# Column sums of image 0's group 0: Pool additions instead of accumulating transfers, and one lane-us more ahead of the sums of image 3's first normalization

## The chip, the cores and the metric

The kernel runs on one core of one Trainium2 chip. The metric is the device time of one execution in microseconds; lower is better. All numbers are for fp32 data.

## The reference

The input x holds four images of 64 x 64 positions with 64 channels. Four layers follow one another:

```python
# layer 0: self-attention over the 4096 positions of an image
q, k, v = x @ Wq + bq, x @ Wk + bk, x @ Wv + bv
x = gamma * einsum('bmn,bmc->bnc', softmax(q @ k.T), v) + x
# layer 1: a gated convolution block
y = dw3x3(ln(x) @ pw1 + b); y = y1 * y2; y = y * (mean(y) @ sca + b)
x = x + (y @ pw2 + b) * beta
z = ln(x) @ pw3 + b; x = x + ((z1 * z2) @ pw4 + b) * gamma
# layer 2: attention of the image with itself, no weights
x = softmax(xf.T @ xf) applied to xf, + x
# layer 3: attention with 32 inner channels, then a normalization over the batch
f = softmax(theta(x) @ phi(x).T); w_y = (f @ g(x)) @ W + b
x = x + gamma * (w_y - mean) / sqrt(var + eps) + beta
```

Layer 1 thus has two normalizations over channels for every image (`ln`). In layer 2 the score matrix is symmetric, so that a tile of exponentials computed once can be used a second time, transposed.

## The kernel before, in words

**Order of the work.** Everything runs on one core. The order on TensorE, ScalarE, VectorE and Pool is the order in which the program issues it (a manual schedule). `items` is a list of steps: layer 0 of images 0 to 3 (32 items each), then layer 2 of image 0, then layer 2 and layer 3 of the images in turn. Two *lanes* run beside the items, `conv` (layer 1 of an image) and `misc` (projections, features). A lane is a list of generators. A generator issues some instructions and yields a number of lane-us; the lane issues its next step when its clock, which the items advance by `tick`, has come that far. So a larger yield puts all later steps of a lane later among the items:

```python
def step(self):
    try:
        self.next = max(self.next, self.now - 8.0) + next(self.gens[0])
```

Layer 1 of image 3 begins 34 items after the start of its layer 0, that is in the first items of layer 2 of image 0. There an item advances `conv` by 3.3 lane-us, and by 1.5 in seven items marked `slow`.

**Layer 2 of image 0.** The positions fall into eight groups h of 512. For image 0 the list `PART` gives the tiles of each group; group 0 comes first. Each item n computes one tile of 128 x 1024: four score matmuls (L1391) into a PSUM slot, two exponentials on ScalarE (L1396) into half of a buffer `e` (pool `ep`, six buffers of 2048 columns), and some items later four product matmuls (L1452). Tiles listed in a pair are used twice. For these,

- `turned` transposes the tile on VectorE (L1409) into `turned`;
- `column_sums` adds the tiles of the group: two sums in the halves of a buffer `esum`, by transfers from Pool's queue that accumulate (L1425), one more transfer that adds the halves (L1429), and an addition of 512 columns on Pool (L1433);
- three items after the last tile of a pair `turned_products` issues 64 matmuls (L1478), written to two PSUM slots, and VectorE copies or adds them to `A` (L1493 where `A` is new, else L1491), which frees the slots;
- nine items after the group's last tile `spread_sums` reads `esum` on VectorE (L1441, L1442).

Group 0 has eight such tiles, items 4 to 7 and 10 to 13; group 1 has four, groups 6 and 5 have eight each. In the other images `column_sums` adds on Pool (L1431), and only there.

Three PSUM slots of 1024 columns are in turn for everything here: L1391, L1478 (two at once), and layer 1's matmuls (L1206).

**Layer 1 of image 3, first part.** `norm` squares x on ScalarE (L1165), sums over channels on TensorE (L1171), computes the inverse deviation (L1176, L1177, L1179, L1180), spreads it over the channels by eight transfers on SP's queue (L1184) into `xn`, and multiplies it by x in two halves on VectorE (L1192). Then come four pointwise matmul groups (L1206), each evacuated by ScalarE into `pad` (L1223), and the 3 x 3 taps: the first of nine on ScalarE (L1237), the rest on VectorE (L1241, L1244), for the second half of the channels. A second pass over the same `pad` does the first half (L1206, L1223, L1237, L1241, L1252), and L1258, L1261, L1263, L1265 and L1270 close the block. The second normalization and the second pointwise pair (L1206, L1289, L1291, L1295, L1298) follow.

The yield between the second square and the sums is `first - 2.5` lane-us.

Of the kernel before, what the change touches and what calls it, by code (L numbers as in the profile page):

```python
# [691 lines left out]
def fast_path(ctx: ExitStack, tc: tile.TileContext, a: dict, out: bass.AP, bad):  # L692
    nc = tc.nc
    B, H, W, C = a["x"].shape
# [31 lines left out]
    def new_ps():  # L726
        if turn_of["banks"]:
            if turn_of["bank"] % turn_of["banks"] == turn_of["banks"] - 1:
                turn_of["bank"] += 1
            k = new_bank(), new_bank()  # L730
            return PS[:, 512 * k[0] : 512 * k[0] + 1024]
        s = turn_of["slots"][turn_of["ps"] % len(turn_of["slots"])]
        turn_of["ps"] += 1
        return PS[:, bass.ts(s, 1024)]
# [13 lines left out]
    def new_e(name="e"):  # L748
        return ep.tile([128, 2048], F32, tag="e", name=name)

    def new_t(name="t"):
        return tp.tile([128, 1024], F32, tag="t", name=name)

    def new_big(name):
        return big.tile([128, 4096], F32, tag="big", name=name)
# [404 lines left out]
    def norm(x, y, first, more):  # L1160


        sq = [new_t("sq"), new_t("sq")]
        for i in range(2):
            act(sq[i], x[:, bass.ts(i, 1024)], AF.Square)  # L1165
            yield first - 2.5 if i else 2.5
        ps = new_ps()
        for i, src in enumerate(((x, x), (sq[0], sq[1]))):
            for j in range(4):
                c = 512 * j if i == 0 else 512 * (j % 2)  # L1170
                mm(  # L1171
                    ps[32 * j : 32 * j + 32, bass.ts(i, 512)], jsel, src[j // 2][:, c : c + 512],
                    start=True, stop=True,
                )
        t = new_t()
        act(t[:, 0:512], ps[:, 0:512], AF.Square)  # L1176
        stt(t[:, 0:512], t[:, 0:512], -1.0, ps[:, 512:1024], ALU.mult, ALU.add)  # L1177
        yield 4.0
        act(t[:, 0:512], t[:, 0:512], AF.Ln, bias=eps1)  # L1179
        act(t[:, 512:1024], t[:, 0:512], AF.Exp, scale=-0.5)  # L1180
        yield 3.0
        for j in range(4):
            for h in range(2):
                nc.sync.dma_start(  # L1184
                    out=y[64 * h : 64 * h + 64, bass.ts(j, 512)],
                    in_=t[32 * j + 16 * h : 32 * j + 16 * h + 16, 512:1024]
                    .unsqueeze(1).to_broadcast([16, 4, 512]),
                )
        yield 11.0 + more
        for jp in range(2):  # L1190
            cols = bass.ts(jp, 1024)
            nc.vector.tensor_mul(y[:, cols], y[:, cols], x[:, cols])  # L1192
            yield 1.8
# [6 lines left out]
    def layer1(b):  # L1200
        x = X[:, b]
# [8 lines left out]
                    )  # L1210

        y = xn.tile([128, 2048], F32, tag="xn", name="xn")
        yield from norm(x, y, 4.5, 3.0 if b == B - 1 else 0.0)
        yg = new_big("yg")
        yw = yg.rearrange("c (s q p h) -> c p q s h", s=2, p=2, h=H)
        ysum = sm.tile([128, 8], F32, tag="ysum", name="ysum")
# [108 lines left out]
    def layer2(b, when_free=None):  # L1325


        x, m, first = X[:, b], im[b], len(items)
# [84 lines left out]
        def column_sums(n):  # L1413
            h, _, _, run, _ = steps[n]
            if run is None:
                return
            k, e = mine_t[h].index(n), st["e"][n]
            if k == (0 if b == 0 else 1):
                st["esum"][h] = new_e("esum")
            if h not in st["esum"]:  # L1420
                return
            esum = st["esum"][h][:, 0:1024]
            if b == 0:
                both = st["esum"][h]
                nc.gpsimd.dma_start(  # L1425
                    out=both[:, bass.ts(k % 2, 1024)], in_=e, **({} if k < 2 else {"accum_op": ALU.add})
                )
                if n == mine_t[h][-1]:
                    nc.gpsimd.dma_start(out=esum, in_=both[:, 1024:2048], accum_op=ALU.add)  # L1429
            else:  # L1430
                nc.gpsimd.tensor_add(esum, st["e"][mine_t[h][0]] if k == 1 else esum, e)  # L1431
            if n == mine_t[h][-1]:
                nc.gpsimd.tensor_add(esum[:, 0:512], esum[:, 0:512], esum[:, 512:1024])  # L1433
# [62 lines left out]
        def item(n):  # L1496
            if n in weights_at:
                weights(weights_at[n])
            score(n)
            turned(n)  # L1500
            column_sums(n)
            todo.append(n)
            if n == 2:
# [309 lines left out]
    for b in range(B):  # L1813
        if b:
            misc_to[len(items)] = True
        layer0(b)
        if b + 1 < B:
            gens = [load_x(i) for i in range(1, B)] if b == 0 else []
            misc_from[32 * b + 16] = gens + [project0(b + 1)]
        conv_from[32 * b + 34] = layer1(b)  # L1820
# [241 lines left out]
```

## Time and profile before

| | us |
|---|---|
| median of 3 runs | 2462.84 (2461.17 to 2462.88) |
| profiled execution, whole | 2460.35 |
| its span | 2458.5 |
| TensorE busy (share of the span) | 2419.4 (98%) |
| ScalarE busy | 1642.8 (67%) |
| VectorE busy | 1475.9 (60%) |
| Pool busy | 533.0 (22%) |
| granted TensorE clock, mean | 0.997 |
| L1425, 28 issues on Pool | 22.0 |
| L1431, 126 additions on Pool that read `esum` and `e` | 299.5 (2.377 each) |

The page gives times of one profiled execution. The span runs from its first to its last instruction; the whole execution is 1.85 us longer, and the median of the runs is 2.5 us above that. A line such as L1096 is a line of the kernel before. "Busy" of TensorE counts matmuls at whatever clock was granted, so a slow stretch looks busy. Layer 2 of image 0 lies between about 1025 and 1260 us of the span.

### The profile page before, as it was taken

How to read it: one execution, taken by the hardware profiler on the slowest of the kernel's cores; microseconds unless marked ns; L12 is line 12 of the kernel's file. 1: busy time of each engine (PE TensorE's matmuls, PEld its weight loads, DVE VectorE, ACT ScalarE, POOL GpSimd, SP SyncE). 2: the span in 40 equal slices, each digit the busy share in tenths (PEclk: the TensorE clock that was granted, in tenths of full speed). 3: DMA queues.
4: the chain of work that ended last, by engine and by line, in shares of the span. 5: the costliest groups of instructions: out<-in, count | busy, mean ns of one | idle time of the engine just before them, and what ended most of it. 6: DMA issues, size and time to landing. Idle time of an engine off the chain costs nothing.

```text
span 2458.5 us, 63660 instructions
## 1 busy us (share of the span) xinstructions
PE 2419.4 (98%) x27509; PEld 930.3 (38%) x27509; DVE 1475.9 (60%) x1794; ACT 1642.8 (67%) x3140; POOL 533.0 (22%) x383
## 2 busy tenths in 40 slices
PE   9999999999999999999999999999999999999998
PEld 3343453336333633335434442144431344421113
DVE  2010378227822773268656668876668866678886
ACT  4656766676666666668654459954479744579996
POOL 2000000000000000020136551255631365622110
PEclk9999999999999999999999999999999999999999
DMA  3000000000000000250540027610075400286554
GB/s 79 1 18 1 19 1 18 18 19 1 18 18 19 1 19 18 61 113 2 126 83 19 19 64 136 138 28 22 17 149 118 80 20 20 70 169 141 120 117 118
DMA packets 67669, 136.40 MB, mean 55 GB/s; under 512 B 13004, under 2 KB 34229, under 8 KB 67381
## 3 DMA queue, kind: packets, MB, share of 16 engines
q0 software_dynamic: 24320, 86.55, 17.4%
q1 hardware_dynamic: 42309, 43.85, 7.9%
q8 instruction: 218, 3.57, 0.6%
q10 hardware_dynamic: 752, 1.85, 0.2%
q14 instruction: 70, 0.57, 0.1%
HBM read 4.80 MB, written 4.19 MB: 4 GB/s over the span
## 4 chain that ended last, share of the span: by engine, by line
PE 87%; DVE 6%; ACT 4%; issue 1%; SPq 1%; DMA 1%; ACTq 0%; DVEq 0%
PE PS L1096 18%; PE PS L1122 18%; PE PS L1391 9%; PE PS L1452 9%; PE PS L1645 9%; PE PS L1706 8%; PE PS L1478 7%; PE PS L1206 2%; DVE tg L1697 2%; ACT e L1656 2%; ACT e L1396 1%; DVE X L1567 1%; PE PS L1560 1%; PE PS L1171 1%; PE PS L1295 1%
## 5 line engine op out<-in xcount | busy, mean ns | idle before, releaser
L1101 ACT ACTIVATE e<-PS 128x1024 f32<-128x1024 f32 x512 | 523.7, 1023 | 338.7 <-PE PS L1096 305.6
L1396 ACT ACTIVATE e<-PS 128x512 f32<-128x512 f32 x632 | 370.8, 595 | 342.4 <-PE PS L1391 321.5
L1096 PE MATMUL PS<-X,q 64*64 64x512 f32 x4096 | 573.6, 590 | 2.3 <-DVE X L979 1.7
L1122 PE MATMUL PS<-e,vq 64*64 64x512 f32 x4096 | 575.6, 592 | 0.0
L1656 ACT ACTIVATE e<-PS 128x512 f32<-128x512 f32 (+2 forms) x588 | 500.1, 921 | 59.4 <-PE PS L1645 37.9
L1697 DVE TENSOR_TENSOR tg<-tg,e 128x2048 f32<-128x2048 f32 x172 | 393.8, 2290 | 43.1 <-ACT e L1656 31.3
L1391 PE MATMUL PS<-ko 64*64 64x512 f32 x2528 | 340.5, 598 | 1.5 <-ACT ko L1313 0.8
L1452 PE MATMUL PS<-e,X 64*64 64x512 f32 x2528 | 334.8, 592 | 0.5 <-ACT own L1464 0.3
L1241 DVE SCALAR_TENSOR_TENSOR y<-pad,vec,y 128x1024 f32<-128x1024 f32 x240 | 309.8, 1291 | 18.7 <-ACT y L1237 11.3
L1431 POOL TENSOR_TENSOR esum<-esum,e 128x1024 f32<-128x1024 f32 x126 | 299.5, 2377 | 54.3 <-ACT e L1396 47.3
L1409 DVE STREAM_TRANSPOSE turned<-e 128x1024 f32<-128x1024 f32 x196 | 240.5, 1238 | 111.3 <-ACT e L1396 111.1
L1645 PE MATMUL PS<-tg,ph 32*64 32x512 f32 x4096 | 295.7, 613 | 1.7 <-ACT e L1656 0.8
L1096 PEld LDWEIGHTS PS<-X,q 64*64 64x64 f32 x4096 | 183.2, 133 | 261.5 <-issue 181.5
L1122 PEld LDWEIGHTS PS<-e,vq 64*64 64x64 f32 x4096 | 183.1, 133 | 253.7 <-issue 158.1
L1425 POOL DMA_DIRECT2D esum<-e x28 | 22.0, 785 | 1170.7 <-ACT e L1396 1066.7
L1706 PE MATMUL PS<-e,tg 128*32 128x512 f32 x2048 | 272.6, 604 | 0.0
L1109 DVE TENSOR_REDUCE sums<-zs 128x1 f32<-128x4 f32 x128 | 19.6, 153 | 276.2 <-ACT e L1101 276.0
L1452 PEld LDWEIGHTS PS<-e,X 64*64 64x64 f32 x2528 | 104.3, 133 | 168.4 <-issue 145.6
L1678 POOL DMA_DIRECT2D xn<-e x116 | 101.1, 904 | 292.4 <-ACT e L1656 204.6
L1391 PEld LDWEIGHTS PS<-ko 64*64 64x64 f32 x2528 | 97.2, 133 | 162.9 <-issue 138.0
L1645 PEld LDWEIGHTS PS<-tg,ph 32*64 32x64 f32 x4096 | 63.5, 130 | 223.3 <-ACT e L1656 190.9
L1396 ACT ACTIVATION_READ_ACCUMULATOR e<-PS 128x1 f32 x632 | 127.4, 202 | 0.0
(219 smaller groups left out, 1727.5 us busy)
## 6 DMA issues: line engine op xcount, KB each, us to landing
xn<-e POOLq DMA_DIRECT2D x132, 512.0 KB, 5.3
esum<-e POOLq DMA_DIRECT2D x28, 512.0 KB, 5.8
xn<-t SPq DMA_DIRECT2D x64, 128.0 KB
ph<-tg SPq DMA_DIRECT2D x64, 128.0 KB
xn<-X SPq DMA_DIRECT2D x224, 32.0 KB
xr<-X SPq DMA_DIRECT2D x176, 32.0 KB
ko<-ko SPq DMA_DIRECT2D x32, 128.0 KB
xr<-in_x_dram SPq DMA_DIRECT2D x13, 256.0 KB
```

The source lines that it names most:

```text
L1096: mm(ps[64 * c : 64 * c + 64, bass.ts(r, 512)], m.q[rows_, 128 * t + 64 * c : 128 * t + 64 * c + 64], x[rows_, bass.ts(g, 512)], start=Tru ...
L1101: act(es[g // 2][:, bass.ts(g % 2, 1024)], ps, AF.Exp, bias=SHIFT0, accum_out=zs[:, g : g + 1],)
L1122: ins = mm(PS[64 * s : 64 * s + 64, 2048 + 512 * j : 2560 + 512 * j], vq[rows_, :], es[j // 2][rows_, k : k + 512], start=t == 0 and i < 2 ...
L1241: stt(y1, win, wt, y1, ALU.mult, ALU.add)
L1391: mm(ps[64 * c : 64 * c + 64, bass.ts(r, 512)], m.ko[rows_, k : k + 64], m.ko[rows_, bass.ts(h, 512)], start=True, stop=True,)
L1396: act(e[:, bass.ts(r, 512)], ps[:, bass.ts(r, 512)], AF.Exp, bias=SHIFT2, accum_out=slot(g, 2 * u + r),)
L1431: nc.gpsimd.tensor_add(esum, st["e"][mine_t[h][0]] if k == 1 else esum, e)
L1452: mm(st["acc"][r][64 * c : 64 * c + 64, :], xw[rows_, 4 * g + 2 * u + c, :], st["e"][n][rows_, bass.ts(c, 512)], start=n == mine[h][0], st ...
L1645: mm(PS[64 * c : 64 * c + 64, bass.ts(banks[k], 512)], m.ph[32 * k : 32 * k + 32, 128 * mc + 64 * c : 128 * mc + 64 * c + 64], m.th[32 * k ...
L1656: act(e[:, 512 * lo : 512 * k], PS[:, 512 * banks[lo] : 512 * banks[lo] + 512 * (k - lo)], AF.Exp,)
L1697: nc.vector.tensor_add(esum, esum, e)
L1706: mm(st["y"][32 * k : 32 * k + 32, :], m.gx[:, i % 32, :], es[i][:, bass.ts(k, 512)], start=mc == 0, stop=i % 32 == 31,)
```

## The change

Group 0 of image 0 takes the path of the other images: its first tile issues nothing, its second allocates `esum` and adds the first two tiles on Pool, and the others are added one by one. Groups 1, 6 and 5 keep their transfers. In `norm` of image 3's first normalization, the yield ahead of the sums is 3.0 instead of 2.0 lane-us. Below L1417 every line of the changed kernel has a number one higher.

```diff
         y = xn.tile([128, 2048], F32, tag="xn", name="xn")
-        yield from norm(x, y, 4.5, 3.0 if b == B - 1 else 0.0)
+        yield from norm(x, y, 5.5 if b == B - 1 else 4.5, 3.0 if b == B - 1 else 0.0)
...
             k, e = mine_t[h].index(n), st["e"][n]
-            if k == (0 if b == 0 else 1):
+            moved = b == 0 and h > 0
+            if k == (0 if moved else 1):
                 st["esum"][h] = new_e("esum")
             if h not in st["esum"]:
                 return
             esum = st["esum"][h][:, 0:1024]
-            if b == 0:
+            if moved:
                 both = st["esum"][h]
                 nc.gpsimd.dma_start(
                     out=both[:, bass.ts(k % 2, 1024)], in_=e, **({} if k < 2 else {"accum_op": ALU.add})
                 )
                 if n == mine_t[h][-1]:
                     nc.gpsimd.dma_start(out=esum, in_=both[:, 1024:2048], accum_op=ALU.add)
             else:
                 nc.gpsimd.tensor_add(esum, st["e"][mine_t[h][0]] if k == 1 else esum, e)
```

## Prediction

> **What bounds the kernel now.** I read the page first, for the engine that fills the span and for the chain that ended last.
>
> ```profile
> PE 2419.4 (98%) x27509; PEld 930.3 (38%) x27509; DVE 1475.9 (60%) x1794; ACT 1642.8 (67%) x3140; POOL 533.0 (22%) x383
> ...
> PE 87%; DVE 6%; ACT 4%; issue 1%; SPq 1%; DMA 1%; ACTq 0%; DVEq 0%
> ```
>
> TensorE is busy for 98% of the span and owns 87% of the chain. An edit on Pool or in the order of the lane can therefore only pay where TensorE waits or runs slowly. So I cut the stretch of the change (the first items of image 0's layer 2) into windows. Columns: busy time and count of each engine, granted clock, DMA share, GB/s.
>
> ```profile
> 1044.00:1049.00 5.00, 4.77 (x140) 3.07 (x136) 2.35 (x2) 0.75 (x3) 0.86 (x1) 1.00 1.02 203
> 1049.00:1054.00 5.00, 0.61 (x4) 0.30 (x8) 2.56 (x6) 1.09 (x4) 0.86 (x1) 0.78 0.74 138
> 1054.00:1059.00 5.00, 5.00 (x28) 1.42 (x24) 1.14 (x1) 1.55 (x3) 0.00 (x0) 0.54 0.08 16
> ```
>
> TensorE works 0.61 us of the second window, and in the third it is "busy" at a clock of 0.54. In windows of 5 us over the whole span, the clock falls nowhere else between start and end. TensorE's timeline gives the size:
>
> ```profile
> 1047.68 1.09 PE L1391 MATMUL PS<-ko 64*64 64x512 f32 x8
> 1053.38 1.99 PE L1206 MATMUL PS<-xn,pw 64*64 64x512 f32 x8 [4.62 <-DVE A L1493]
> 1055.14 1.93 PE L1452 MATMUL PS<-e,X 64*64 64x512 f32 x8
> 1056.85 1.92 PE L1391 MATMUL PS<-ko 64*64 64x512 f32 x8
> 1058.56 1.08 PE L1206 MATMUL PS<-xn,pw 64*64 64x512 f32 x8
> ```
>
> It stands for 4.62 us. The three groups after that take 1058.56 - 1053.38 = 5.18 us, where three groups at full clock take 3 x 0.86 = 2.58 (0.86 is a group's step in the chain). Together 4.62 + 2.60 = **7.2 us**. VectorE's timeline and the chain tell why:
>
> ```profile
> 1044.60 1.25 DVE L1409 STREAM_TRANSPOSE turned<-e 128x1024 f32<-128x1024 f32 x1 [6.34 <-ACT e L1396]
> 1045.77 1.18 DVE L1192 TENSOR_TENSOR xn<-xn,X 128x1024 f32<-128x1024 f32 x1
> 1051.44 1.23 DVE L1192 TENSOR_TENSOR xn<-xn,X 128x1024 f32<-128x1024 f32 x1 [4.48 <-DMA xn<-t]
> 1052.58 1.41 DVE L1493 COPY A<-PS 128x256 f32<-128x256 f32 x4
> ```
>
> ```profile
> 1037.45 2.46 SPq L1184
> 1039.95 1.99 SPq L1184
> ...
> 1041.98 2.00 SPq L1184
> 1044.03 7.21 DMA xn<-t
> ...
> 1052.66 0.68 DVE A L1493 x2
> ```
>
> The second product of the normalization (L1192) waits for the last broadcast transfer (L1184). The four copies L1493 stand behind it in VectorE's queue, though their matmuls (L1478) ended at 1047.7. The copies hold two of the three PSUM slots, the score matmuls L1391 the third, so L1206 has no slot.
>
> **What the Trainium skill says.** "TensorE: Matmul & The Clock Gate", Part 1 (The HAM clock gate): after an idle window of about 3.4 us the array drops to half rate, and needs about as long busy to come back. The trace agrees: 4.62 us idle, then 5.2 us at about half speed; idle pieces near 1 us elsewhere in this layer leave the clock at 1.00. "DMA: Bandwidth & Descriptors", Issuing engines are not separate DMA queues: transfers of SP and of Pool share the same 16 engines. It agrees: beside the esum transfers the share is 1.02, and single SP issues of L1184 last up to 2.46 us against a median of 0.60. "SBUF — State Buffer", Who interferes with whom: a VectorE instruction with two SBUF inputs and a Pool instruction that reads SBUF exclude each other. It agrees, with Pool's line first:
>
> ```profile
> 1271.72 12.46 POOL L1431 TENSOR_TENSOR esum<-esum,e 128x1024 f32<-128x1024 f32 x5 [2.45 <-ACT e L1396]
> ```
> ```profile
> 1274.70 2.38 DVE L1298 TENSOR_TENSOR X<-X,t 128x512 f32<-128x512 f32 x1 [0.19 <-ACT t L1296]
> ```
>
> L1298 takes 0.69 us when Pool is idle (at 1261.06); here it waited out the add.
>
> **Part one, the column sums.** Group 0 has 8 tiles. Eight L1425 transfers and one L1429 go, 9 x 512 KB; seven L1431 adds come, and the half add L1433 stays. Pool's issues, 9 x about 0.8 = 7 us, become 7 x 2.37 (median of the L1431 row) = 16.6 us of adds. In this stretch Pool has nothing else to do, and a tile's item takes TensorE 3 x 0.86 = 2.58 us, so Pool keeps up: the last add ends about one item after its tile. What hides them is Pool's idle time. Three things follow.
> (a) L1184 loses its competitors. Eight issues at 0.60 from 1034.7 end near 1039.6 and, with the 5.3 us that the esum transfers take to land, are there by 1045 (an estimate), where they landed at 1051.2.
> (b) The half add no longer meets the taps L1241. Before, it took 2.21 us at 1074.4 against 1.27 alone, and a pair of taps 3.49 against 2.60. VectorE gains 0.9 us, off the path.
> (c) Both products L1192 read two SBUF inputs and meet an add each.
>
> **Part two, one lane-us.** The instruction order of the changed kernel shows that the sums (L1171) stay at their place on TensorE. What moves is the second L1192: from ahead of the four copies L1493 to behind them and the next transpose L1409, one item later. The four L1206 of the first pass stay. Later lane steps slide by one item: some L1237 on ScalarE, the four L1206/L1223 of the second pass, and pieces of the second pointwise pair (L1206, L1291, L1295) at the end. SP's order is unchanged; Pool's differs only by part one.
>
> **The new timetable**, from durations above. Tile 10 is exponentiated at 1044.6; its add runs to 1047.0. The first L1192 waits for it and ends near 1048.1 (1047.0 + 1.2). The copies follow at once, L1478 having ended; the first slot is free after two of them, as in the chain (0.68 us): 1048.9. TensorE would be there at 1048.6. So L1206 stands 0.3 us instead of 4.62, and the clock stays up. Tile 11 is ready at 1050.1; its add runs to 1052.7, the second L1192 to 1053.9. Its first reader, the third L1206, comes six groups after 1048.9, at 1054.1: just in time. The second L1206, at 1058.56 before, comes at 1048.9 + 2.58 = 1051.5: **7.0 us earlier**. ScalarE could take it back, being busy 4.93 of 5 us from 1059 on, but its item (two exponentials and two L1223) runs at the 2.58 us of TensorE's, and its own idle times here (5.3 us ahead of the first L1223, 2.0 after it) were caused by the same stall.
>
> **The slid steps.** The second pass's last L1223 moves one item later, but L1237 now follows it directly instead of after a pair of exponentials; the taps of the second pass start where they did (1134.4 before), and VectorE runs from there without idle time to L1258 at 1184.1, whose reader L1261 comes at 1186.4: 2.2 us of cover. If the taps slipped by a whole item, 2.6 us, L1261 and L1270 would stand for 0.4 to 2.2 us. I take 0. The pieces at 1255 to 1310 move around idle times of 0.39 and 0.64 us; bounds -1 to +1, I take 0.
>
> **Sum.** -7.2 + 0.3 = -6.9 us, bounds -8.5 to -3.5. The profiled execution took 2460.35 us (span 2458.5 and 1.85 around it), giving 2453.4; the median of the runs is 2.5 us above it, 2462.84, giving **2455.9**, -0.28%. A measurement of this kernel can tell about 0.2%, 4.9 us.
>
> **Rivals.** *The stall moves.* If the second L1192 waits for two adds, or the transposes are late, it ends near 1056.2 and the third L1206 stands about 2.1 us, too short for the clock to drop. Gain 6.9 - 2.1 = 4.8, 2458.0. For it: the margin above is 0.2 us. Against it: between adds Pool waits for its tile, so VectorE gets its turn. With a slip of the second pass too, 2460.
> *The wait was not the DMA's or the order's.* If the slot is freed late for another reason, the gap stays: 2462. Against it: the copies started within 0.1 us of L1192's end.
> *The adds hold VectorE back (slower).* If the adds lag and reach into the taps L1241 of the first pass, each overlap costs up to 2.4 us, and that pass has no slack: at 1128.2 ScalarE's L1223 waited 0.53 us for its end. Beyond three overlaps, 7.1 us, the gain is gone; all seven cost 16.6, giving 2472. Against it: by the timetable the last add and the half add end near 1059 and the taps begin near 1062.
> *The edit does less than it says*: the sums do not move, but the second L1192 does, so this is settled.
>
> **How the numbers follow.** Forecast 0.70 (mostly 2454 to 2457.5), moved stall 0.18 (2457.5 to 2460.5, a third of it still beyond 0.2%), unchanged 0.06, slower 0.06, of which 0.05 beyond 0.2%. Faster by over 0.2%: 0.69 + 0.05 = 0.74; slower 0.05; the rest 0.21. The range 2453.5 to 2460 leaves out the last two and the tails.
>
> **What would show it.** Right: no TensorE idle time over 1 us and no window with a clock under 0.95 near 1045 to 1060; short SP issues of L1184; L1493 ahead of the second L1192; first-group taps near 1062; everything after 1070 some 7 us earlier. Wrong: an idle time ahead of the third L1206 or of L1478, taps of 2.4 us or more beside L1431, or a new idle time at L1261 or L1270.

## The result, and the profile after

| | before | changed |
|---|---|---|
| median of 7 runs, us | 2461.17 (2457.23 to 2464.43) | 2452.37 (2451.54 to 2456.51) |
| profiled execution, us | 2460.35 | 2456.51 |
| its span, us | 2458.5 | 2454.7 |

The ratio is **0.9972, 95% interval 0.9962 to 0.9981**: faster, and by what was forecast (-0.28%). (Ratios and intervals here are computed from the single runs; the quotient of the two medians above is 0.9964.) The profiled execution of the changed kernel happens to be the longest of its seven. So the profile after tells how the stall went, but its total is about 4 us too long; the first experiment below repeats the same program.

The page of the changed kernel, engines and chain. TensorE is 2.4 us less busy, and less of the chain is DMA's and SP's:

```profile
PE 2417.0 (98%) x27509; PEld 916.3 (37%) x27509; DVE 1479.3 (60%) x1794; ACT 1644.3 (67%) x3140; POOL 540.9 (22%) x381
...
PE 86%; DVE 8%; ACT 4%; issue 1%; SPq 0%; DMA 0%; DVEq 0%; ACTq 0%
```

The windows of the stretch (busy time and count of PE, PEld, DVE, ACT, POOL, then the granted clock, DMA share, GB/s). In the second window TensorE works 4.88 us instead of 0.61, the clock stays at 1.00 in all three, and the DMA engines are empty:

```profile
1044.00:1049.00 5.00, 5.00 (x148) 3.13 (x142) 3.18 (x2) 1.27 (x4) 2.37 (x1) 1.00 0.01 3
1049.00:1054.00 5.00, 4.88 (x44) 1.53 (x48) 4.38 (x7) 3.59 (x9) 2.36 (x1) 1.00 0.01 2
1054.00:1059.00 5.00, 5.00 (x52) 1.98 (x48) 3.29 (x3) 4.88 (x13) 4.51 (x2) 1.00 0.02 5
```

TensorE's timeline (start, us, line): no idle time stands before any of these lines, and a group takes 1.04 to 1.09 us, not 1.99. From L1391 to the first L1206 it is 1.21 us where the next step is 0.91: the 0.3 us of the timetable.

```profile
1048.89 1.09 PE L1391 MATMUL PS<-ko 64*64 64x512 f32 x8
1050.10 1.09 PE L1206 MATMUL PS<-xn,pw 64*64 64x512 f32 x8
1051.01 1.04 PE L1453 MATMUL PS<-e,X 64*64 64x512 f32 x8
...
1052.72 1.04 PE L1206 MATMUL PS<-xn,pw 64*64 64x512 f32 x8
...
1055.30 1.04 PE L1206 MATMUL PS<-xn,pw 64*64 64x512 f32 x8
```

VectorE's timeline, with Pool's behind it. The copies (L1494, the L1493 of before) now start when the *first* product ends, and the second product comes behind the next transpose. Each product takes 2.4 us instead of 1.18, because an addition of Pool is running when it starts; it ends 1.1 us after that addition (1049.38 after 1048.29, 1054.89 after 1053.80):

```profile
1046.98 2.40 DVE L1192 TENSOR_TENSOR xn<-xn,X 128x1024 f32<-128x1024 f32 x1
1049.30 1.40 DVE L1494 COPY A<-PS 128x256 f32<-128x256 f32 x4
1051.33 1.25 DVE L1409 STREAM_TRANSPOSE turned<-e 128x1024 f32<-128x1024 f32 x1 [0.62 <-ACT e L1396]
1052.50 2.39 DVE L1192 TENSOR_TENSOR xn<-xn,X 128x1024 f32<-128x1024 f32 x1
```
```profile
1045.92 2.37 POOL L1432 TENSOR_TENSOR esum<-esum,e 128x1024 f32<-128x1024 f32 x1 [3.94 <-ACT e L1396]
1051.44 2.36 POOL L1432 TENSOR_TENSOR esum<-esum,e 128x1024 f32<-128x1024 f32 x1 [3.14 <-ACT e L1396]
...
1059.65 1.27 POOL L1434 TENSOR_TENSOR esum<-esum 128x512 f32<-128x512 f32 x1
```

SP's queue: the eight issues of the broadcast (L1184) take 5.72 us in all, where they took 11.21 before.

```profile
1035.92 5.72 SPq L1184 DMA_DIRECT2D xn<-t  x8
```

**How later gains are counted.** Starts scatter: the matmuls L1478 just ahead of the stage begin between 1043.7 and 1045.3 in the fourteen profiles, whatever the edit: the sums L1171 stand 17.5 us ahead of it in every one. So I take every later mark from that L1478 and subtract the same distance in the kernel before. One example, the next L1478, in TensorE's timelines of the kernel before and of the first experiment:

```profile
1044.04 3.71 PE L1478 MATMUL PS<-turned,xr 32*64 32x256 f32 x128
...
1069.01 3.71 PE L1478 MATMUL PS<-turned,xr 32*64 32x256 f32 x128
```
```profile
1044.65 3.71 PE L1478 MATMUL PS<-turned,xr 32*64 32x256 f32 x128
...
1062.52 3.71 PE L1478 MATMUL PS<-turned,xr 32*64 32x256 f32 x128
```

(1069.01 - 1044.04) - (1062.52 - 1044.65) = 24.97 - 17.87 = **7.10 us** gained. The marks named by their time in the profile before are: *1069* (that L1478), *1192* (1192.32, the L1478 after the first L1270), *1247* (1246.92, L1478), *1286* (1285.93, the L1391 after the L1478 of 1280.75); at 1462, the first L1645, all stand as at 1286 within 0.1 us.

| kernel | 1069 | 1192 | 1247 | 1286 |
|---|---|---|---|---|
| changed (profiled run) | 7.09 | 6.30 | 3.84 | 4.69 |
| e1 changed, repeated | 7.10 | 6.31 | 6.29 | 8.21 |
| e2 Pool part only | 5.95 | 5.94 | 5.92 | 5.92 |
| e3 lane part only | 7.06 | 6.28 | 6.28 | 8.20 |
| e4 group 0's sums left out | 7.16 | 7.15 | 6.20 | 6.20 |
| e5 second L1192 only moved | 7.10 | 7.10 | 5.44 | 4.41 |
| e6 left out, lane part | 7.34 | 6.56 | 6.56 | 8.48 |
| e7 group 5 on Pool too | 7.09 | 6.31 | 6.29 | 8.20 |
| e8 all groups on Pool | 7.09 | -2.31 | -3.25 | -1.34 |
| e9 second L1192 and late steps | 7.09 | 7.08 | 7.05 | 8.98 |
| e10 late steps only | 1.24 | 1.23 | 0.46 | 2.15 |
| e11 as e5, group 5 on Pool | 7.08 | 7.07 | 7.05 | 7.04 |
| e12 as e9, group 5 on Pool | 7.09 | 7.09 | 7.09 | 8.99 |

Three accounts can be read in it: the stall (7.1 by 1069), a loss of 0.8 between 1069 and 1192 where the lane is later, and a gain of 1.9 to 2.0 between 1247 and 1286 where it is later there. A fourth, a loss just ahead of 1247 or behind it in some executions, is taken up with e5 and e11.

### The profile page after: what moved, and what is told of

Read it like the earlier page. It is cut to its first block, busy times and chain, and to the rows that moved or that the text cites. A ratio compares the mean times of both kernels' runs of the same rounds, so it can differ in the third digit from the quotient of the medians.

```text
span 2454.7 us, 63654 instructions
## 1 busy us (share of the span) xinstructions
PE 2417.0 (98%) x27509; PEld 916.3 (37%) x27509; DVE 1479.3 (60%) x1794; ACT 1644.3 (67%) x3140; POOL 540.9 (22%) x381
## 4 chain that ended last, share of the span: by engine, by line
PE 86%; DVE 8%; ACT 4%; issue 1%; SPq 0%; DMA 0%; DVEq 0%; ACTq 0%
PE PS L1096 18%; PE PS L1122 18%; PE PS L1391 10%; PE PS L1453 10%; PE PS L1646 8%; PE PS L1707 8%; PE PS L1479 7%; DVE tg L1698 3%; PE PS L1206 2%; ACT e L1657 2%; ACT e L1396 1%; DVE X L1568 1%; PE PS L1561 1%; PE PS L1064 1%; PE PS L1171 1%
## 5 line engine op out<-in xcount | busy, mean ns | idle before, releaser
L1391 PE MATMUL PS<-ko 64*64 64x512 f32 x2528 | 335.6, 596 | 2.6 <-DVE u L1291 1.5
L1432 POOL TENSOR_TENSOR esum<-esum,e 128x1024 f32<-128x1024 f32 x132 | 314.0, 2379 | 59.7 <-ACT e L1396 52.4
L1241 DVE SCALAR_TENSOR_TENSOR y<-pad,vec,y 128x1024 f32<-128x1024 f32 x240 | 308.8, 1287 | 18.2 <-ACT y L1237 10.9
L1432 POOL TENSOR_TENSOR esum<-e 128x1024 f32<-128x1024 f32 x22 | 52.2, 2373 | 1206.2 <-ACT e L1396 1187.3
L1453 PEld LDWEIGHTS PS<-e,X 64*64 64x64 f32 x2528 | 98.0, 133 | 176.3 <-issue 156.7
L1391 PEld LDWEIGHTS PS<-ko 64*64 64x64 f32 x2528 | 90.5, 132 | 169.9 <-issue 145.7
```

What stands on the lines that cost most here:

```text
L1241: stt(y1, win, wt, y1, ALU.mult, ALU.add)
L1391: mm(ps[64 * c : 64 * c + 64, bass.ts(r, 512)], m.ko[rows_, k : k + 64], m.ko[rows_, bass.ts(h, 512)], start=True, stop=True,)
L1453: mm(st["acc"][r][64 * c : 64 * c + 64, :], xw[rows_, 4 * g + 2 * u + c, :], st["e"][n][rows_, bass.ts(c, 512)], start=n == mine[h][0], st ...
```

## The experiments

The line numbers of all of them are those of the kernel before. Each ratio is to runs of the kernel before that were taken beside the experiment; the median of those lay between 2459.65 and 2460.88 us, so medians of different experiments can be compared to about 1 us only.

### e1: the changed kernel again

The same program, with one statement put on the line before it so that lines keep their numbers.

```diff
-            k, e = mine_t[h].index(n), st["e"][n]
+            k, e = mine_t[h].index(n), st["e"][n]; moved = b == 0 and h > 0
```

> The changed kernel again, with its lines numbered as before, timed beside the three parts below. All theories: ratio to before 0.997 (gain 6 to 8 us). Theory (VectorE's queue): TensorE stands about 0.3 us ahead of the first L1206, no slow clock.

Measured: 2452.45 us, ratio 0.9965 (0.9951 to 0.9978). No idle time over 0.3 us at the stage, 7.10 us at the mark 1069, 8.21 at the end, just above the 6 to 8 expected. It confirms the size and shows that the slid steps are worth something: 0.8 lost, then 1.9 gained.

### e2: the Pool part alone; e3: the lane part alone

e2 has only the `moved` lines, e3 only this one:

```diff
-        yield from norm(x, y, 4.5, 3.0 if b == B - 1 else 0.0)
+        yield from norm(x, y, 5.5 if b == B - 1 else 4.5, 3.0 if b == B - 1 else 0.0)
```

> Only the Pool additions, lane yields as before: both L1192 stay ahead of the copies L1493. Theory (VectorE's queue): the transfers L1184 land early, so nothing waits for them, but the first L1192 waits for an addition (it ends 1.2 us later than alone) and the second adds 1.2 us, so that the copies start about 1.2 us later than in the changed kernel and TensorE stands 1.2 to 2 us ahead of the first L1206, too short for the clock to drop. Gain 5 to 6 us, ratio about 0.9978. Rival (only the order of the lane pays): stall and slow clock as before, ratio 1.000.

> Only the extra lane-us, transfers as before: the copies L1493 go ahead of the second L1192, which still waits for the late transfer. Theory (VectorE's queue): the first slot is free 0.7 us after L1478 ends, TensorE stands 0.1 us or less, the second L1192 ends near 1052.6 and is in time for the third L1206. Gain 6 to 7.5 us, ratio about 0.997, so that the two parts do not add up: each removes the same stall. Rival (only the transfers' removal pays): SP's issues of L1184 stay long, TensorE waits for the second L1192 at the third L1206 for 2 us or more, ratio 0.999 or above.

Measured: e2 2455.13 us, ratio 0.9981 (0.9975 to 0.9988); e3 2453.22 us, ratio 0.9967 (0.9955 to 0.9979). In e2 the transfers are gone but both products still stand ahead of the copies. VectorE's and TensorE's timelines of e2:

```profile
1046.73 3.53 DVE L1192 TENSOR_TENSOR xn<-xn,X 128x1024 f32<-128x1024 f32 x2
1050.19 1.40 DVE L1493 COPY A<-PS 128x256 f32<-128x256 f32 x4
```
```profile
1050.98 1.09 PE L1206 MATMUL PS<-xn,pw 64*64 64x512 f32 x8 [1.25 <-DVE A L1493]
```

The two products last 3.53 us (one of them held by an addition), the copies start 1.1 us later than in the changed kernel (5.19 us after the start of their L1478, against 4.05), and TensorE waits 1.25 us. The clock stays up, so 5.95 us are gained rather than 7.1. In e3 it is the other way: the broadcast is as slow as before (second line), the second product still waits for it (first line) and ends at 1053.50, not near 1052.6 as expected. That is only just in time for the third L1206:

```profile
1052.27 1.23 DVE L1192 TENSOR_TENSOR xn<-xn,X 128x1024 f32<-128x1024 f32 x1 [1.25 <-DMA xn<-t]
```
```profile
1034.36 11.16 SPq L1184 DMA_DIRECT2D xn<-t  x8
```
```profile
1053.60 1.21 PE L1206 MATMUL PS<-xn,pw 64*64 64x512 f32 x8
```

The third L1206 comes 0.97 us after its predecessor where the usual step is 0.86, so about 0.1 us is lost there. In the changed kernel the second product ends 0.4 us ahead of it (1054.89, 1055.30). So **the parts do not add**: either removes the same stall, the lane part nearly all of it (7.06 us) and without touching a transfer, but without any margin.

### e4: the column sums of group 0 left out

No transfer and no addition for group 0; a memset stands for its sums. Order as before.

```diff
+            if b == 0 and h == 0: return nc.gpsimd.memset(esum[:, 0:512], 1.0) if n == mine_t[h][-1] else None
```

> The kernel before with the column sums of group 0 left out (a memset stands for them): no transfers, no additions, order of the lane as before. It tells the competition for the DMA engines from everything else. Theory: L1184 lands before the first L1192 needs it, both L1192 run back to back at 1.2 us each, the copies start within 0.5 us of the end of L1478, TensorE stands under 1 us. Gain 6.5 to 7.5 us, ratio about 0.997. Rival (the transfer L1184 is late by itself, from its own chain): it still lands near 1051, the stall stays, ratio 1.000.

Measured: 2454.25 us, ratio 0.9973 (0.9965 to 0.9981). The broadcast takes 5.84 us, the two products follow one another in 2.32 us, the copies start at 1049.17, and no stall over 0.3 us is left: 7.16 us at 1069. With no lane edit there is no loss by 1192 and no gain by 1286; the 0.95 us lost ahead of 1247 come again under e5.

```profile
1046.93 2.32 DVE L1192 TENSOR_TENSOR xn<-xn,X 128x1024 f32<-128x1024 f32 x2
1049.17 1.41 DVE L1493 COPY A<-PS 128x256 f32<-128x256 f32 x4
```

With e2 and e3 this shows both ends of the cause: the transfers made the second product late, and the queue carried it to the copies.

### e5: only the second L1192 moves

The changed kernel, but the yield after the second product gives the lane-us back.

```diff
-            yield 1.8
+            yield 0.8 if jp and first == 5.5 else 1.8
```

> The whole change, but the lane's later steps are given their old due times: of image 3's first normalization only the second L1192 falls later, by one lane-us; the column means, the matmuls L1206 after the first pair and all later steps of the lane stand as before the change. Theory (the stall is VectorE's queue and nothing else, the slid later steps are a separate small account): no stall over 0.4 us ahead of the first L1206; 7.1 us gained by the next L1478 as with the whole change; then neither the 0.8 us that the whole change loses between 1084 and 1187 (L1452 behind the copy L1464: 0.31 as before, not 0.83, and none of 0.27) nor the 2.0 us that it gains between 1247 and 1281 (L1295 0.39, L1452 0.2 and L1478 at 4.3 as before). Total 6.6 to 7.2 us, about 2454, ratio 0.997 to 0.9975. Rival (the slid steps are part of how the stall goes): the stall comes back by 1 us or more ahead of the first L1206, total 6 us or less. Rival (the 2.0 us at 1247 to 1281 come from the earlier stage's timing, not from the slid steps): they are gained here too, total 8 us or more, ratio 0.9965 or less.

Measured: 2454.49 us, ratio 0.9983 (0.9976 to 0.9990). Up to 1192 it is as expected: 7.10 and no 0.8 lost. The end, 4.41 in the trace, was expected only for the case that the stall comes back, and it did not. Instead two losses came later in its profiled execution, 1.66 us by 1247 and 1.03 by 1286. TensorE's timeline of e5:

```profile
1237.85 0.64 PE L1452 MATMUL PS<-e,X 64*64 64x512 f32 x2 [0.59 <-issue]
...
1255.47 1.08 PE L1295 MATMUL PS<-u,pw 128*64 128x512 f32 x4 [1.42 <-DVE u L1291]
```

The first is a pause within a group, for which the trace shows no releaser. The second has a cause in the trace. Pool's half addition of group 5, which starts when that group's last transfer has landed, meets VectorE's two additions L1467. They take 2.45 us instead of 1.42, and L1291 and L1295 behind them are late by as much (1.42 us of waiting instead of 0.39). VectorE's timeline and Pool's:

```profile
1251.77 2.45 DVE L1467 TENSOR_TENSOR A<-own,A 128x512 f32<-128x512 f32 x2 [4.21 <-ACT own L1464]
```
```profile
1251.68 1.27 POOL L1433 TENSOR_TENSOR esum<-esum 128x512 f32<-128x512 f32 x1 [3.71 <-DMA esum<-esum]
```

In e1 the half addition starts at 1252.42, 0.27 us after L1467 has ended at 1252.15; in e3, e4 and e10 it misses it by 0.02 to 0.16 us. So a pause that delays L1467 and not the transfers can bring the second loss with it.

The same places cost the changed kernel's profiled run 1.37 and 1.46 us of waiting (its L1467 take 2.49), and a pause of 0.75 to 0.93 us, without the second loss, can be computed from the pitch of the L1478 (12.2 to 12.4 us instead of 11.5) in e4 and e10. In four of ten profiles with group 5's transfers there is such a pause, whatever the edit. So e5's total does not tell what its order is worth; e11 has the same order with less load on the transfers.

### e6: the sums left out, with the lane part

As e4, and the lane edit.

> Column sums of image 0's group 0 are left out (a memset stands for them), with the lane edit as in the whole change. Theory (the Pool's add holds VectorE back by port, 0.3 us at the edge of PE's stall, no more): the first L1192 takes 1.2 us and not 2.4, the copies L1493 start a us earlier, and the 0.3 us ahead of the first L1206 is gone or the same; total within 0.6 us of the whole change's, ratio 0.9960 to 0.9968. Rival (Pool's adds cost more than that, by their ports or by what they hold up later): 1.5 us or more faster than the whole change, ratio 0.996 or less.

Measured: 2453.29 us, ratio 0.9975 (0.9967 to 0.9983). The first product takes 1.18 us, and the copies no longer wait for it but for their matmuls:

```profile
1046.04 1.18 DVE L1192 TENSOR_TENSOR xn<-xn,X 128x1024 f32<-128x1024 f32 x1
1048.09 1.42 DVE L1493 COPY A<-PS 128x256 f32<-128x256 f32 x4 [0.87 <-PE PS L1478]
```

7.34 us at 1069 against 7.10: being held back by Pool's additions costs the change **0.24 us** on the path. The ratio came out above the expected 0.9960 to 0.9968, though the gain in the trace (8.48) is as expected; between times that were not taken side by side, 1 us decides nothing.

### e7: groups 0 and 5 on Pool

```diff
+            k, e = mine_t[h].index(n), st["e"][n]; moved = b == 0 and h not in (0, 5)
```

> The whole change, and image 0's group 5 (its adds fall at 1214 to 1253) on Pool as well. In that stretch the DMA engines are 0.93 to 1.04 busy and PE waits 0.8, 0.9 and 0.65 us ahead of L1391 and L1310. Theory: these waits are for ScalarE's and VectorE's copies L1313 behind PE's own transposes, not for transfers, so they stay and the time is that of the whole change within 1 us, ratio 0.996 to 0.9972; the instruction L1314 on SP, 16.3 us long now, is below 12. Rival (PE waits there for ko by transfer): the three waits fall by half or more, 1.5 to 2.5 us more gained, ratio 0.9955 or less. Rival (the lock that made L1192 2.4 us long slows the 1.25 us transposes L1409 and the copies L1313 there): the waits grow, 1 us or more is lost, ratio 0.997 or more.

Measured: 2452.83 us, ratio 0.9974 (0.9965 to 0.9983). The three waits stand unchanged at 0.82, 0.94 and 0.66 us, the issues of L1314 take 12.28 us against 16.29 in e1 (below 12 was expected), and the gain is 8.20: those waits are for the copies L1313, not for transfers. (The ratio lies just above the range expected with that; the gain in the trace, equal to e1's, does not.) The two L1192 of the second normalization are held by additions here as well, 4.60 us for two against 2.31, but in a gap of VectorE.

### e8: all groups of image 0 on Pool

```diff
+            k, e = mine_t[h].index(n), st["e"][n]; moved = False
```

> The whole change, and all of image 0's groups on Pool, group 1 (1062 to 1110, beside the taps L1241 and L1244 of image 3's first convolution) and the group at 1171 to 1211 too. Theory of the slower case that the prediction left at 5 in 100: Pool's adds hold back VectorE where it runs in full. If an add lets no VectorE tensor instruction of two SBUF operands run beside it, seven adds of 2.4 us during the taps put the taps back by up to 16 us; the lane has slack there, so PE loses 0 to 8 us: ratio 0.997 to 0.9995. Rival (scalar_tensor_tensor at 1.28 us runs beside Pool's adds without delay): L1241 stays at 1.3 us, ratio 0.9960 to 0.9970.

Measured: 2462.95 us, ratio **1.0014** (1.0006 to 1.0021): slower than before, and beyond the upper end that was expected. Group 0's gain is there (7.09), and 9.4 us are lost by 1192 (0.8 of them by the slid steps). Pool's timeline and VectorE's, at group 1:

```profile
1076.15 3.13 POOL L1431 TENSOR_TENSOR esum<-e 128x1024 f32<-128x1024 f32 x1 [15.21 <-ACT e L1396]
1079.36 2.69 POOL L1431 TENSOR_TENSOR esum<-esum,e 128x1024 f32<-128x1024 f32 x1
```
```profile
1075.81 1.24 DVE L1241 SCALAR_TENSOR_TENSOR y<-pad,vec,y 128x1024 f32<-128x1024 f32 x1
1076.97 1.24 DVE L1409 STREAM_TRANSPOSE turned<-e 128x1024 f32<-128x1024 f32 x1
1078.13 4.47 DVE L1244 SCALAR_TENSOR_TENSOR yg<-pad,vec,y 128x512 f32<-128x512 f32 x2
```

Whichever comes second waits: the addition behind a tap (3.13 us instead of 2.37), then the two L1244 behind the additions (4.47 us instead of 1.42). A transpose is not held. The next transpose is late, and so TensorE stands 2.15 us ahead of L1478. The group at 1180 is worse, since a chain of small steps lies there (L1252, L1258, L1263, L1265, then L1270 on TensorE), with an L1467 among them that takes 2.64 us instead of 0.69. VectorE's and TensorE's timelines and the windows of e8:

```profile
1180.06 2.83 DVE L1252 SCALAR_TENSOR_TENSOR yg<-y,yg 128x512 f32<-128x512 f32 x1
...
1190.33 1.67 DVE L1265 TENSOR_SCALAR pw2s<-pw,ch 128x64 f32<-128x64 f32 x1
```
```profile
1192.05 1.97 PE L1270 MATMUL PS<-yg,pw2s 128*64 128x512 f32 x4 [3.90 <-DVE pw2s L1265]
```
```profile
1190.00:1195.00 5.00, 2.95 (x12) 0.60 (x12) 3.23 (x5) 0.78 (x1) 1.94 (x1) 0.59 0.21 53
1195.00:1200.00 5.00, 5.00 (x128) 3.11 (x128) 0.57 (x1) 0.00 (x0) 0.00 (x0) 0.73 0.18 43
```

L1265 takes 0.25 us elsewhere. TensorE stands 3.90 us, and the clock falls to 0.59 and 0.73: L1270 takes 1.97 us, against 1.08 in e1. The slower rival of the prediction is a real mechanism; group 0 is only not where it strikes.

### e9: the second L1192 and the late steps; e10: the late steps alone

e9 is e5 with one lane-us added after the last L1277 of image 3; e10 is the kernel before with that line alone.

```diff
-            yield 3.0
+            yield 4.0 if b == B - 1 and j == 3 else 3.0
```

> As the kernel in which only the second L1192 moves, and one lane-us more is put after the last L1277 of image 3's first pointwise output, so that the second normalization and the steps L1206, L1291, L1295 of the gated half fall one lane-us later, as they do in the whole change, while the taps L1241 and the steps up to L1277 stand as before the change. Theory (three separate accounts: the stall 7.1 gained, the slid taps 0.8 lost, the slid gated half 2.0 gained): 7.1 us gained at the L1478 of 1186, as there; then L1452 behind L1467 no longer 0.2 late, that L1478 3.7 and not 4.3 us long, L1391 behind L1493 0.3 and not 0.64; together 2 us: 9.1 us at the first L1645, time 0.8 below the whole change's, ratio 0.9957 to 0.9970. Rival (the 2.0 us hang on the slid taps as well): total 7.1 us or less, ratio 0.9972 or more, as with the second lane step alone.

> The kernel before, and the one lane-us after the last L1277 alone: neither the transfers nor the second L1192 are touched. Theory (the late gain is an account of its own): the stall of 4.6 us and the half clock stand as before at 1049 to 1058, nothing is gained up to the L1478 of 1247, and 1.9 to 2.0 us between it and the first L1391 after the next but one L1478 (the one of 1281): ratio 0.9988 to 0.9996. Rival (it is gained only when the earlier stage has been shortened): 0 us, ratio 0.9996 to 1.0004.

Measured: e9 2452.00 us, ratio 0.9969 (0.9957 to 0.9981); e10 2458.95 us, ratio 0.9993 (0.9985 to 1.0001). In the table e9 keeps the 7.1 to 1247 and gains 1.93 behind it. e10 gains 1.69 there, 2.15 - 0.46, with the early stall left in place. The 1.24 at 1069 is scatter of that stall: 4.38 us idle in this execution for 4.62 before, and the slow clock ends after two groups instead of three (1057.60 - 1054.25 = 3.35 us, for 5.18). TensorE's timeline of e10:

```profile
1054.25 1.99 PE L1206 MATMUL PS<-xn,pw 64*64 64x512 f32 x8 [4.38 <-DVE A L1493]
1056.01 1.76 PE L1452 MATMUL PS<-e,X 64*64 64x512 f32 x8
1057.60 1.03 PE L1391 MATMUL PS<-ko 64*64 64x512 f32 x8
```

So the 7.1 us of the table holds against the one profile of before; against this one, the same stall is worth 5.9. The 0.8 lost and the 2 gained are accounts of their own; the times alone do not tell e10 from no change.

Where the 2 us lie is seen in TensorE's timelines. Before, behind the first gated output:

```profile
1259.07 1.08 PE L1295 MATMUL PS<-u,pw 128*64 128x512 f32 x4 [0.39 <-DVE u L1291]
1260.08 1.09 PE L1391 MATMUL PS<-ko 64*64 64x512 f32 x8
1260.99 1.04 PE L1206 MATMUL PS<-xn,pw 64*64 64x512 f32 x8
...
1265.29 1.07 PE L1452 MATMUL PS<-e,X 64*64 64x512 f32 x2
1266.55 1.51 PE L1452 MATMUL PS<-e,X 64*64 64x512 f32 x11 [0.19 <-DVE A L1467]
```

and in e1:

```profile
1253.39 1.09 PE L1391 MATMUL PS<-ko 64*64 64x512 f32 x8 [0.39 <-DVE u L1291]
1254.41 1.08 PE L1295 MATMUL PS<-u,pw 128*64 128x512 f32 x4
```

In the later order the score group goes ahead of L1295, ScalarE has its tile a group earlier, and the L1467 behind that tile's transpose is no longer late. Before, two matmuls of L1452 fill the 1.26 us from 1265.29 to 1266.55; eight take 0.86 elsewhere, so about 1.05 us are lost. The L1478 at 1280.75 took 4.31 us and takes 3.71 in e1 (0.60); the wait ahead of the L1391 at 1286 was 0.64 and is 0.28 (0.36). Sum 2.01; the table has 1.92.

The 0.8 us lost are two waits of L1452 for a ScalarE copy. In e1:

```profile
1098.49 1.95 PE L1452 MATMUL PS<-e,X 64*64 64x512 f32 x16 [0.83 <-ACT own L1464]
1153.92 1.95 PE L1452 MATMUL PS<-e,X 64*64 64x512 f32 x16 [0.27 <-ACT own L1464]
```

Before, the first is 0.31 and the second is not there. The tap L1237 (1.24 us) has slid on ScalarE towards L1464: at the first wait it stands directly ahead of it, at the second with two exponentials between, where there were two and four before. e5, e9, e11 and e12, which leave the taps where they were, have 0.31 to 0.32 and no second wait.

### e11 and e12: e5 and e9 with group 5 on Pool

The `moved` line of e7 in both.

> The kernel in which only the second L1192 moves, with image 0's group 5 on Pool as well as group 0. In that kernel's own profile TensorE paused at 1237.85 (0.59 us, no releaser shown) and 1.42 us ahead of L1295; the DMA engines are full there, and eight L1425 of group 5 are among their load. Theory (the pause comes of that load): no pause, the two L1478 ahead of 1247 stand 11.5 us apart and not 13.1, L1295 waits 0.39; gain 7.1 at the first L1645, a median 1 to 2 us below that of the kernel with the second L1192 alone, ratio 0.9967 to 0.9977. Rival (the pause is not the load's): it comes here too, total 4.4 to 5.5 us, ratio 0.998 or more.

> The kernel with the second L1192 and the late steps moved, with image 0's group 5 on Pool as well: all that was found to pay together. Theory: 9.0 us gained at the first L1645, no pause near 1237 in the profiled run, runs that lie within 2 us of one another, ratio 0.9958 to 0.9970. Rival (group 5's adds hold VectorE back where the gated half is near): L1192 at 1237 is 4.6 us long for two and the steps after it slip, 8 us or less.

Measured: e11 2453.30 us, ratio 0.9974 (0.9964 to 0.9983); e12 2452.36 us, ratio 0.9966 (0.9955 to 0.9977). Neither profile has the pause: the L1478 stand 11.5 us apart, L1295 waits 0.40 in e11, and the gains are 7.04 and 8.99. The second loss of e5 cannot come here, since group 5's half addition runs at 1238.75 in e11, far ahead of the L1467 of 1250.28, which takes 1.42 us. For the pause within the group the cause stays open. Profiles without group 5's transfers (e7, e8, e11, e12) had it in none of four, those with them in four of ten. That fits the load of transfers but is too few to show it, and one of e11's ten runs still took 2456.83 us. The versions e9 and e12 have the largest gain in the trace (9.0); their times cannot be told from the changed kernel's.

## Why the prediction was right

**The bound and the stall.** Right in place, cause and size: 4.62 us idle and half a clock after it, called 7.2, minus 0.3; measured 7.1 (5.9 against e10's profile, where the slow clock ended sooner). e2, e3 and e4 undo one link each and every one leaves what the theory says, but for the later end of e3's second product.

**The timetable.** On the axis of the profile before, which the changed kernel's trails by 1.21 us at L1478: the first L1192 ends at 1048.2 (predicted 1048.1), L1206 starts at 1048.9 (1048.9), the second L1192 ends at 1053.7 (1053.9; the prediction's own 1050.1 + 2.37 + 1.2 make 1053.7), the third L1206 starts at 1054.1 (1054.1), taps begin at 1061.9 (near 1062), and the half addition ends at 1059.7 (near 1059). The margin ahead of the third L1206, called 0.2 us, was 0.4, so the moved stall did not come.

**Transfers.** That L1184 would lose its competitors was right (11.21 to 5.72 us); e3 shows that it was not needed once the lane part is there, though without it the second product is only just in time. The prediction treated the two parts as one cure and did not say that either would do.

**The slid steps** are the term that was mis-sized. It was taken as 0. Its fear, L1261 and L1270 standing 0.4 to 2.2 us, did not come about; ScalarE's copy L1464 behind a slid L1237 did, 0.8 us, which the prediction named as moved and did not price. The pieces of the second pointwise pair brought 1.9 to 2.0 us, outside the bounds of -1 to +1, since the prediction counted only the idle times that the trace marks and not L1452 and L1478 stretched by waits within a group. Net 1.1 us in favour: the forecast sum was 6.9, e1's trace has 8.2.

**The total.** Forecast 2455.9 from a median of 2462.84. In the comparison the kernel before had 2461.17, which is 1.7 us of the difference to 2452.37; the slid steps are 1.1; the rest is within the scatter of the runs. The median of 2452.37 lies 1.1 us below the range of 2453.5 to 2460, and the two medians are 8.8 us apart, just beyond the bound of 8.5; the ratio 0.9972 on 2462.84 gives 2455.9. That it meets the forecast to the last digit is luck: the sum lacked the 1.1 us, two of the seven runs are 3 to 4 us longer than the other five, and e1 has 0.9965. (In the chances, a third of 0.18 is 0.06, where 0.05 was added.)

**The slower rival** was rightly given little for this edit, and e8 shows its mechanism where additions do meet the lane. It was named for the taps L1241, and there e8 decides nothing: no tap starts while an addition runs (they keep 1.24 to 1.29 us, and one addition waits behind a tap). L1244, L1252, L1265, L1277 and L1467 pay. That a tap can be held too is seen in the kernel before, in the pair of 3.49 us that the prediction names. The same mechanism, with a half addition and L1467, is the second loss of e5 and of the changed kernel's profiled run; the prediction did not see that one.

## What to carry to other kernels

A wait in an in-order queue is paid by whatever stands behind it: look first for the instruction behind the waiting one that has long been ready, and let it go first, before making the waited-for thing faster. Two edits that each remove the same stall do not add, and a due time that is moved slides every later step of its lane, so price these too, also by matmul groups that merely take longer than usual. An addition moved to Pool is free only while VectorE is not on the path.

## What the runs showed of the hardware

- A VectorE product with two SBUF inputs takes 1.18 us alone and 2.39 when an addition of Pool began 1.1 us ahead of it: whichever starts second waits for the other. In e8 even a small scaling of 128 x 64 grows from 0.25 to 1.67 us, while transposes keep 1.24. I had expected the first, not that so small an instruction pays.
- The clock of TensorE fell after idle times of 3.90, 4.38 and 4.62 us, and not after 1.25 or 2.15. That agrees with the window of about 3.4 us that the Trainium skill states ("TensorE: Matmul & The Clock Gate", Part 1: The HAM clock gate). What I had not expected is how much a gap just past it adds: after the 3.90 us in e8, L1270, the L1452 behind it and the L1478 behind that lost 0.9 us each (1.97 for 1.08, 1.99 for 1.09, 4.57 for 3.71). How long the clock stays low is not fixed: 5.18 us after the 4.62, 3.35 after the 4.38, so that the "about as long" of the prediction fits e10 and not the kernel before.
- The issuing of transfers itself becomes slow beside others: eight issues of L1184 on SP take 11.2 us beside Pool's transfers (DMA share 1.05 between 1039 and 1044) and 5.7 without them (0.83 in the profile after).
